# A ring of their own for the late experts' outputs, in a two-layer metaformer kernel on one core

## The chip, the core and the metric

The kernel runs on one core of a Trainium2 chip. A core has five engines with queues of their own: the tensor engine (PE; its weight loads are shown apart as PEld), the vector engine (DVE), the scalar engine (ACT), GpSimd (POOL) and the sync engine (SP), which here only issues transfers. Sixteen DMA engines move data between the chip's memory and the core's working memory. Each engine works through its instructions in the order in which the program gives them, and waits on semaphores for the others.

The metric is the time of one execution in device microseconds, as the median of the runs shown. A profiled execution gives the trace.

## The reference

The input is 32 images of 56 x 56 tokens with 128 channels. Two layers follow each other, each with a mixing step and a step of experts, and each adds its result to the tokens:

```
# layer 0
x = x + conv3x3(sign(batchnorm(ln(x))), sign(W) * scale)          # 128 -> 128 channels
t = t + sum over the 2 best of 8 experts of gate * (ln(t) @ expert_w[e] + expert_b[e])
# layer 1
a = sigmoid((y @ Wa1 + ba1) * (y @ Wa2 + ba2));  b likewise         # y = ln(x), 16 channels
z[i, j, c] = sum over k of a[i, k, c] * b[k, j, c]                  # per image and channel
x = x + sigmoid(y @ Wg + bg) * (ln(z) @ Wz + bz)
# experts that choose tokens: 64 experts, each takes the 8 best tokens of each image
logits = ln(t) @ gate_w.T + gate_b;  probs = softmax over the tokens of an image
top 8 tokens per image and expert, weights topv
pooled = sum over the 8 of topv * token
o = gelu([pooled, 1] @ weight1[e]) ; o = [o, 1] @ weight2[e]
t[chosen token] += topv * o
```

The last step is the one that matters here. An expert makes one output row of 128 numbers per image, and this row, times eight weights, is added to eight tokens of that image. Two experts may choose the same token, so additions to one image's tokens must follow each other.

## The kernel before, in words

**Tiles and stages.** A unit is 896 tokens, held as 128 partitions x 7 x 128 numbers (448 KB). Two images make a pair of seven units; there are sixteen pairs. A first pass over all units (`fetch1`, `stats1`, `norm1`) gathers the batch statistics and stores the turned, normalised units. Then each pair passes through convolution (`sign`, `conv`, `conv_back`), the eight gated experts (`moe_turn`, `moe_route`, `moe_gates`, `moe_experts`, `moe_add`), the product of a and b (`tri_turn`, `tri_b`, `tri_a`, `tri_z`, `tri_out`) and the choice of tokens (`gate_stats`, `gate_turn`, `gate_logits`, `top8`, `pool_rows`). Consecutive pairs overlap.

**The gated experts.** `moe_experts` handles one seventh of a unit. SP loads the eight gates, spread over the partitions, into a tile of 512 KB (L821, tag `gb`, five of them). DVE multiplies the tile by the turned tokens `xT` (L827), and PE multiplies it by the eight experts' weights into one bank (L832). `moe_add` adds the bank to the tokens (L844). A turned unit `xT` is alive from `moe_turn` until its seventh multiply.

**The late experts.** `late_experts` handles four of the 64 experts of the last step at a time, in sixteen groups, and is run twice: with `alone` false for the first thirteen pairs, whose choices are known while the last three pairs are still being worked on, and with `alone` true for the last three pairs, at the end. A group loads its weights (L1412, L1414), multiplies (L1479), turns (L1503), applies gelu (L1519), multiplies again (L1525), adds the bias (L1533) and stores four rows of outputs per image (L1541). For the first thirteen pairs the rows are then loaded again, each repeated eight times, so that one partition holds one chosen token's row (L1551). The images are split into two lots, one of 14 and one of 12 images, so a load covers 112 or 96 partitions. A tile of outputs holds the four experts of a group for one lot. DVE multiplies the whole tile by the weights (L1558), and POOL adds each expert's rows to the output in memory by an indirect transfer that accumulates (L1575). Within a lot each of these 64 transfers waits for the one before; between lots POOL puts a small memset (L1316).

**The rings.** Every tile belongs to a tag, and a tag has a fixed number of buffers in a ring. Tokens `x` have 15, turned units `xT` have 4, `gb` has 5. The outputs of the late experts take `xT` buffers, so do some of the late experts' weights in the last stage; other weights go to `x` and `gb` buffers, and the first fourteen `alone` experts use other memory that has become free by then (`places`).

**The order.** The program doesn't give its instructions in the order in which its stages are written. Every stage puts operations into a list, with an engine, an estimated time, what it reads and writes, and for a transfer how long it takes to land (`land`). The table `TICK` gives each stage of a pair its place within a period of 14. The planner `Order.run` then walks through a modelled time: an engine that is free takes the operation of lowest place whose inputs are there and whose tiles have a buffer. The order that comes out is fixed in the program, queue by queue; on the chip, engines only wait for each other. So a change of `land`, of the rings or of `TICK` can move instructions on all queues and in all pairs.

Of the kernel before, what the change touches and what calls it, by code (L numbers as in the profile page):

```python
# [17 lines left out]
ALU = mybir.AluOpType  # L18
# [9 lines left out]
C = 128  # L28
N7 = 7
UT = N7 * 128  # L30
NU = 7
# [7 lines left out]
    "fetch": (1.58, 3.45, 5.52, -1.97, 9.89, 8.41, 11.94),  # L39
    "sign": (-0.24, 0.69, 0.62, 6.29, 6.36, 10.44, 7.52),  # L40
    "conv": (1.26, 2.47, 6.82, 8.46, 10.49, 11.27, 13.74),
    "conv_back": (3.04, 3.74, 6.89, 9.11, 10.54, 11.48, 14.87),
    "moe_turn": (4.55, 4.08, 9.93, 10.17, 12.05, 12.07, 15.21),
    "moe_gates": (7.93, 6.46, 10.3, 10.32, 15.22, 13.8, 15.72),
    "moe_experts": (10.11, 8.23, 10.44, 10.38, 15.35, 13.82, 17.26),
    "moe_add0": (14.4, 13.58, 10.89, 13, 17.91, 16.49, 17.47),
    "moe_add1": (12.35, 12.05, 11.31, 12.55, 16.09, 14.74, 18.98),
    "tri_turn": (16.03, 16.94, 19.18, 18.34, 19.2, 18.97, 19.62),
    "moe_stats": (4.06, 9.6, 11.95, 15.11),
    "moe_route": (6.11, 10.25, 12.5, 15.67),  # L50
    "tri_stats": (14.43, 14.07, 18.68, 19.34),
    "tri_b": (20.52, 21.37),
    "tri_a": (22.17, 21.41),
    "tri_z": (22.19,),
    "tri_out": (23.45, 23.11, 25.14, 25.06, 25.81, 28.13, 29.03),
    "gate_stats": (23.81, 25.31, 26.89, 30.24),
    "gate_turn": (25.22, 25.8, 26.84, 28.27, 29.66, 32.16, 31.08),
    "gate_logits": (26.8, 27.15, 28.55, 30.19, 30.4, 34.44, 34.71, 34.72),
    "clear": (32.94,),
    "top8": (36.55,),  # L60
    "pool_rows": (39.18,),
    "late_first": (27.19, 27.47, 30.26, 33.5, 37.45, 38.24, 40.16, 41.35, 43.38, 44.86, 45.85,
        48.06, 49.55, 51.3, 58.28, 60.22),
    "late_alone": (47.43, 50.82, 50.84, 53.47, 61.88, 67.39, 57.81, 65.6, 63.21, 71.67, 75.8,
        82.21, 97.17, 84.67, 68.82, 79.34),
    "last_sums": (70.63, 74.49, 77.96),
    "last_load": (68.66, 101.21),
    "last_rows": (91.82, 76.74, 99.71, 103.42, 119.45, 116.33),
# [4 lines left out]
NX, NY = 15, 6  # L73
# [212 lines left out]
def kernel(ctx: ExitStack, tc: tile.TileContext, a: dict, out: bass.AP):  # L286
    nc = tc.nc
# [117 lines left out]
    with ExitStack() as c2:  # L405
# [184 lines left out]
        def fetch(p, u):  # L590
# [3 lines left out]
            @op("SP", 360, w=parts(x_), land=1200)  # L594
            def _():
                nc.sync.dma_start(x_.ap, x_units[g])
# [1557 lines left out]
```

## Time and profile before

| what | value |
|---|---|
| median of 3 runs | 3786.38 us (3786.0 to 3797.89) |
| profiled execution | 3805.24 us |
| its span, first to last instruction | 3803.4 us |
| PE busy | 3427.8 us (90%) |
| DVE busy | 3191.5 us (84%) |
| ACT busy | 2350.5 us (62%) |
| POOL busy | 443.8 us (12%) |
| mean DMA rate | 221 GB/s |

The sum of the prediction is made against the profiled execution, and the difference is carried over to the median. In the profile, a group of instructions is named by its line, engine, operation, and output and input tiles. A wait is given as who waited, for whom, how many microseconds in total, how many times, and the longest. "SPq" and "DVEq" are the queues' own instructions; a DMA named as releaser is a transfer that had to land. A row of the timeline starts with its start and length in microseconds, and ends, in brackets, with the idle time of the engine before it and what ended it. In a matmul row of 32-bit data each matmul is counted twice. The granted clock is that of PE, 1.00 being full speed. The profile marks some idle time "issue", for which it shows no wait.

### The profile page before, as it was taken

To read this page: it belongs to the slowest core of one execution; us is meant where nothing else is said; L and a number is where in the kernel's file an instruction comes from. 1 tells how busy PE (TensorE), PEld (TensorE's weight loads), DVE (VectorE), ACT (ScalarE), POOL (GpSimd) and SP (SyncE) were. 2 spreads that over 40 slices of the span, in tenths; PEclk is the share of its full clock that TensorE was granted. 3 is DMA by queue.
4 is the path that set the end of the run, shared out by engine and by line. 5 is a ranking of instruction groups with operands and counts; after the bars stand their busy time and mean duration, and the time that the engine had idled before them with its cause. 6 is when DMAs were issued, how large, how long until landed. Compare 5 with 4: busy or idle time off the path is not lost.

```text
span 3803.4 us, 79485 instructions
## 1 busy us (share of the span) xinstructions
PE 3427.8 (90%) x28051; PEld 2791.8 (73%) x28051; DVE 3191.5 (84%) x10626; ACT 2350.5 (62%) x5438; POOL 443.8 (12%) x506
## 2 busy tenths in 40 slices
PE   7998999999999999999999999999999997876644
PEld 7886878787877777777777777777777775664422
DVE  7997979898989898989898989898989886765551
ACT  6997357575757666666666666666666664453420
POOL 0000000101010101010101010101010104234454
PEclk9999999999999999999999999999999998898667
DMA  7996747474747474747474747474747477687685
GB/s 292 358 356 226 256 155 268 151 272 148 276 150 268 146 268 153 269 154 269 154 269 156 265 155 268 157 267 158 265 160 262 163 251 210 201 248 227 184 238 163
DMA packets 358127, 842.03 MB, mean 221 GB/s; under 512 B 89169, under 2 KB 133154, under 8 KB 357730
## 3 DMA queue, kind: packets, MB, share of 16 engines
q1 hardware_dynamic: 298658, 719.02, 54.8%
q10 hardware_dynamic: 38080, 99.57, 6.6%
q0 software_dynamic: 20992, 18.37, 2.9%
q8 instruction: 223, 3.65, 0.4%
q14 instruction: 174, 1.43, 0.1%
HBM read 661.53 MB, written 175.23 MB: 220 GB/s over the span
## 4 chain that ended last, share of the span: by engine, by line
PE 44%; DVE 27%; DMA 14%; ACT 8%; issue 3%; SPq 2%; POOL 1%; another core or an unknown queue 0%; ACTq 0%; POOLq 0%; DVEq 0%
PE acc L832 21%; DMA gb<-gate 7%; DVE gb L827 5%; DVE stln L488 5%; PE gram L1799 4%; PE ps_cv L633 4%; PE tr L477 3%; PE ps_g L1067 2%; ACT yt L562 2%; DVE frame L611 2%; DVE x L575 2%; DMA w_True<-in_L_ffn_weight 2%; PE ps_z L976 2%; DVE x L1111 1%; DVE sg L1102 1%
## 5 line engine op out<-in xcount | busy, mean ns | idle before, releaser
L832 PE MATMUL acc<-expert_w,gb 128*128 128x128 f32 x12544 | 1473.6, 278 | 73.0 <-DVE gb L827 49.2
L832 PEld LDWEIGHTS acc<-expert_w,gb 128*128 128x128 f32 x12544 | 1437.7, 193 | 121.7 <-DVE gb L827 51.4
L827 DVE TENSOR_TENSOR gb<-gb,xT 128x1024 f32<-128x1024 f32 x784 | 949.3, 1220 | 95.3 <-DMA gb<-gate 91.3
L488 DVE BATCH_NORM_STATS2 stln<-x 128x6 f32<-128x128 f32 x2352 | 600.1, 287 | 1.9
L562 ACT ACTIVATE yt<-x,rmln 128x128 f32<-128x128 f32 x784 | 327.2, 495 | 203.6 <-DVE rmln L550 190.0
L562 ACT ACTIVATE yl<-x,rmln 128x128 f32<-128x128 f32 x756 | 324.2, 494 | 175.7 <-DVE rmln L547 125.3
L633 PE MATMUL ps_cv<-frame,w_sign 128*128 128x448 bf16 x2016 | 420.0, 357 | 8.3 <-DVE frame L611 8.3
L562 ACT ACTIVATE ym<-x,rmln 128x128 f32<-128x128 f32 x784 | 324.6, 486 | 66.9 <-DVE rmln L550 57.3
L633 PEld LDWEIGHTS <-w_sign 128*128 128x128 bf16 x2016 | 196.5, 98 | 174.4 <-DVE frame L611 8.5
L1222 POOL DMA_INDIRECT rows<-y,near x128 | 133.2, 1041 | 995.5 <-DVE k L738 795.7
L1575 POOL DMA_INDIRECT out<-eo_False,picked x128 | 198.1, 1548 | 317.1 <-DMA out<-eo_False,picked 137.0
L1118 POOL MEMSET a_bd<- 128x2048 f32 x15 | 27.1, 1807 | 1655.4 <-PE ps_zo L1089 1655.4
L562 ACT ACTIVATE y<-x,rm 128x128 f32<-128x128 f32 x448 | 210.5, 716 | 14.5 <-DVE rm L547 14.5
L1067 PE MATMUL ps_g<-wg,yT 128*128 128x128 f32 x1568 | 211.2, 283 | 0.0
L1067 PEld LDWEIGHTS ps_g<-wg,yT 128*128 128x128 f32 x1568 | 192.0, 195 | 20.5 <-issue 12.0
L583 ACT COPY xT<-trm 128x512 f32<-128x512 f32 x224 | 110.1, 529 | 151.6 <-PE trm L477 132.7
L641 ACT ACTIVATE cv<-ps_cv,cv_shift,cv_scale 128x448 f32<-128x448 f32 x224 | 159.2, 726 | 70.7 <-PE ps_cv L633 36.1
L844 DVE TENSOR_TENSOR x<-acc,x 128x512 f32<-128x512 f32 (+1 forms) x224 | 139.7, 623 | 73.7 <-PE acc L832 62.8
L1799 PE MATMUL gram<-y 128*128 128x128 f32 x1568 | 198.4, 279 | 0.0
L1799 PEld LDWEIGHTS gram<-y 128*128 128x128 f32 x1568 | 194.4, 200 | 0.5 <-issue 0.5
L488 DVE BATCH_NORM_STATS2 st<-x 128x6 f32<-128x128 f32 x784 | 179.6, 282 | 4.6 <-DMA x<-in_x 4.6
L583 ACT COPY ylT<-trl 128x512 f32<-128x512 f32 x224 | 113.7, 533 | 111.4 <-PE trl L477 102.0
(263 smaller groups left out, 5439.5 us busy)
## 6 DMA issues: line engine op xcount, KB each, us to landing
gb<-gate SPq DMA_DIRECT2D x784, 512.0 KB
x<-in_x SPq DMA_DIRECT2D x224, 448.0 KB
y<-yT SPq DMA_DIRECT2D x112, 448.0 KB
ys<-y SPq DMA_DIRECT2D x112, 448.0 KB
out<-x ACTq DMA_DIRECT2D x105, 448.0 KB
y<-yl ACTq DMA_DIRECT2D x105, 448.0 KB
w_False<-in_L_ffn_weight SPq DMA_DIRECT2D x128, 256.0 KB
w_True<-in_L_ffn_weight SPq DMA_DIRECT2D x102, 256.0 KB
```

Source lines behind the costliest of these rows:

```text
L488: nc.vector.bn_stats(st.ap[:, c0 + k, :], src.ap[:, k, :])
L562: nc.scalar.activation(dst.ap[:, k, :], src.ap[:, k, :], AF.Identity, bias=m, scale=r)
L583: nc.scalar.copy(t.ap[:, n0 : n0 + k, :].rearrange("c n p -> c (n p)"), ps.ap[:, : k * 128],)
L633: nc.tensor.matmul(acc, lhsT=w_sign[:, tap, :], rhs=frames[f][:, 8 * band + kh : 8 * band + kh + 8, kw : kw + W], start=(tap == 0), stop=( ...
L641: nc.scalar.activation(cv.ap[:, :, 64 * h : 64 * h + 64], ps.ap[:, :448].rearrange("c (q n) -> c n q", n=N7), AF.Identity, bias=cv_shift, ...
L827: nc.vector.tensor_tensor(gb.ap, gb.ap, over(xT.ap[:, n, :], E0), ALU.mult)
L832: nc.tensor.matmul(acc.ap[:, n % 4 * C : (n % 4 + 1) * C], lhsT=gb.ap[:, e, :], rhs=expert_w[:, e * C : (e + 1) * C], start=(e == 0), stop ...
L844: nc.vector.tensor_tensor(dst, acc.ap[:, : k * C], dst, ALU.add)
L1067: nc.tensor.matmul(psg.ap[:, n * C : (n + 1) * C], lhsT=yT[:, n0 + n, 16 * u : 16 * u + 16, :].rearrange("c r v -> c (r v)"), rhs=wg, star ...
L1222: nc.gpsimd.indirect_dma_start(out=rows.ap[:, j, :], out_offset=None, in_=y3_d[p], in_offset=bass.IndirectOffsetOnAxis(ap=near.ap[:, k + j ...
L1575: ins = nc.gpsimd.indirect_dma_start(out=tokens_out, out_offset=bass.IndirectOffsetOnAxis(ap=picked[lot][:rows, e : e + 1], axis=0), in_=e ...
L1799: nc.tensor.matmul(gram.ap[:, :C], lhsT=y.ap[:, n, :], rhs=y.ap[:, n, :], start=(g % G16 == 0 and n == 0), stop=(g % G16 == G16 - 1 and n ...
```

## The change

Four things are changed together.

- The outputs of each late expert get a tile of their own, [128, 2, 128] numbers, 1 KB per partition, with both lots in it, under a new tag `eo` with eight buffers. So a group has four tiles with two loads each, in place of two tiles with four loads each. DVE multiplies each expert and lot by itself, with one weight per partition, so there are 128 multiplies of 128 elements in place of 32 of 512. The 128 accumulating transfers stay.
- Token tiles `x` go from 15 buffers to 14, turned units `xT` from 4 to 3.
- Many estimates of `land` are changed.
- `TICK` has new values in every row, and the order of all queues is drawn up anew from it.

The instructions of PE stay the same in kind and number. The core of the diff:

```diff
 TICK = {
-    "fetch": (1.58, 3.45, 5.52, -1.97, 9.89, 8.41, 11.94),
-    "sign": (-0.24, 0.69, 0.62, 6.29, 6.36, 10.44, 7.52),
-    "conv": (1.26, 2.47, 6.82, 8.46, 10.49, 11.27, 13.74),
+    "fetch": (-0.52, 2.15, 5.26, -2.24, 9.7, 8.97, 10.97),
+    "sign": (-0.11, 0.84, 1.3, 6.88, 7.6, 9.29, 7.72),
+    "conv": (1.51, 1.9, 7.02, 8.48, 10.38, 10.64, 13.69),
...
-NX, NY = 15, 6
+NX, NY, NEO = 14, 6, 8
...
-            "x": NX, "u": NY, "ps": 8, "gb": 5, "xT": 4, "yl": 3,
+            "x": NX, "u": NY, "ps": 8, "gb": 5, "xT": 3, "yl": 3, "eo": NEO,
...
-            @op("SP", 360, w=parts(x_), land=1200)
+            @op("SP", 360, w=parts(x_), land=1262)
...
-            @op("SP", 360, r=[("gd", p, u)], w=[gb], land=1300)
+            @op("SP", 360, r=[("gd", p, u)], w=[gb], land=1392)
...
-            @op("SP", 360, r=[pt], w=[("pooled", p)], land=1500)
+            @op("SP", 360, r=[pt], w=[("pooled", p)], land=5600)
...
-                @op("SP", 360, r=[] if alone else [("ph", name)], w=[second_w[j][1]], land=700)
+                @op("SP", 360, r=[] if alone else [("ph", name)], w=[second_w[j][1]], land=868)
...
-            for lot in () if alone else (0, 1):
-                i0, i1 = LOTS[lot]
-                rows = (i1 - i0) * K1
-                eo = new("xT", [128, N7, C], f"eo_{name}_{lot}")
-
-                @op("SP", 720, r=[("o_d", g)], w=[eo], land=300)
-                def _(eo=eo, i0=i0, i1=i1, rows=rows):
-                    for j in range(NE):
+            for j in () if alone else range(NE):
+                eo = new("eo", [128, 2, C], f"eo_{name}_{j}")
+
+                @op("SP", 720, r=[("o_d", g)], w=[eo], land=800)
+                def _(j=j, eo=eo):
+                    for lot in range(2):
+                        i0, i1 = LOTS[lot]
                         nc.sync.dma_start(
-                            eo.ap[:rows, j, :],
+                            eo.ap[: (i1 - i0) * K1, lot, :],
                             o_d[g][j, i0:i1, :].unsqueeze(1).to_broadcast([i1 - i0, K1, C]),
                         )
-                @op("DVE", 600, r=[("picked", p) for p in range(i0 // 2, i1 // 2)], w=[eo])
-                def _(eo=eo, lot=lot, rows=rows):
-                    nc.vector.tensor_tensor(
-                        eo.ap[:rows, :NE, :], eo.ap[:rows, :NE, :],
-                        along(gains[lot][:rows, es], C), ALU.mult,
-                    )
-
-                for j in range(NE):
+                for lot in range(2):
+                    i0, i1 = LOTS[lot]
+                    rows = (i1 - i0) * K1
+                    e = g * NE + j
+
+                    @op("DVE", 200, r=[eo] + [("picked", p) for p in range(i0 // 2, i1 // 2)],
+                        w=[(eo, lot)])
+                    def _(eo=eo, lot=lot, rows=rows, e=e):
+                        nc.vector.tensor_scalar(
+                            eo.ap[:rows, lot, :], eo.ap[:rows, lot, :],
+                            gains[lot][:rows, e : e + 1], None, ALU.mult,
+                        )
                     @op(
-                        "POOL", 2000, land=4000,
+                        "POOL", 2000, land=4200,
...
-                            in_=eo.ap[:rows, j, :], in_offset=None, compute_op=ALU.add,
+                            in_=eo.ap[:rows, lot, :], in_offset=None, compute_op=ALU.add,
```

The other changes of `land`: transfers of a whole unit 1200 to 1262; the store of z 300 to 1150 and its loads back 300 to 800; the late experts' weights 700 to 868 (two at a time 1400 to 1736), their pooled tokens 300 to 450, their bias 100 to 450, the store of their outputs 200 to 450.

## The prediction

> **What bounds the kernel now.** I read the windows first, then the waits of the tensor engine in two stretches, then the waits of the queue and of the vector engine in the late one, then the timeline of one event there.
>
> The windows answer, for the late stretch up to the last pair's token choice, for the rest, and for twelve pairs in the middle (columns: stretch and its length; busy us and instructions of PE, PEld, DVE, ACT, POOL; granted clock; DMA share; GB/s):
>
> ```profile
> 3100.00:3652.00 552.00, 393.98 (x3110) 297.80 (x3106) 333.84 (x1038) 273.00 (x548) 209.81 (x235) 0.82 0.75 221
> 3652.00:3804.00 152.00, 73.12 (x753) 40.20 (x752) 50.38 (x154) 20.68 (x34) 73.83 (x110) 0.72 0.64 179
> 700.00:3000.00 2300.00, 2207.16 (x18188) 1810.91 (x18187) 2101.43 (x6599) 1507.32 (x3375) 146.41 (x126) 1.00 0.60 211
> ```
>
> In the middle PE is the bound: 2207 of 2300 us, clock 1.00. One pair takes 191.8 us (from the first z product of one pair, at 2052.25, to that of the next, at 2244.05), so it loses 92.8 / 12 = 7.7 us. DVE at 2101 is close behind. From 3100 on no engine is full: PE idles 158 us before 3652 and 79 us after it.
>
> PE's waits in the middle (700 to 3000 us; total us, times, longest):
>
> ```profile
> PE acc L832 <- DVE gb L827: 18.6, 28, 1.3
> PE trg L797 <- DVE k L779: 14.4, 11, 1.4
> PE acc L832 <- DVE q_ln L517: 13.3, 12, 1.1
> PE tr_b L477 <- ACT lines L903: 12.6, 12, 1.1
> PE tr_a L477 <- ACT lines L903: 10.2, 24, 0.7
> PE ps_z L976 <- issue: 7.9, 12, 0.7
> PE trg L797 <- DVE gg L783: 7.1, 14, 0.8
> ```
>
> Nearly all of a pair's loss is PE waiting for DVE's gated copies (2.7 us), for the gates (1.8 us), and around the turned a/b lines (2.6 us). These places repeat in every pair, so a new order moves them thirteen times.
>
> The late stretch, first SP's waits, then DVE's (from 3050 us), then one event:
>
> ```profile
> SPq L1551 <- DMA out<-eo_False,picked: 51.3, 7, 9.7
> ```
> ```profile
> DVE eo_False L1558 <- DMA eo_False<-o: 51.6, 17, 13.1
> DVE gb L827 <- DMA gb<-gate: 31.7, 25, 3.4
> ```
> ```profile
> 3150.91 1.61 POOL L1575 DMA_INDIRECT out<-eo_False,picked  x1 [4.07 <-DMA out<-eo_False,picked]
> ...
> 3154.71 3.18 SPq L1551 DMA_DIRECT2D eo_False<-o  x4
> ...
> 3159.75 0.69 DVE L1558 TENSOR_TENSOR eo_False<-eo_False,gains 96x512 f32<-96x512 f32 x1 [7.49 <-DMA eo_False<-o]
> ...
> 3163.49 2.93 PE L832 MATMUL acc<-expert_w,gb 128*128 128x128 f32 x12 [8.97 <-DVE gb L827]
> ```
>
> A scatter keeps its turned tile; the next load of expert outputs waits for it in SP's queue; DVE, which works in its written order, waits 7.5 us for that load; PE then waits 9.0 us for the gated copy that stood behind it on DVE.
>
> **The change, part by part.** PE gets the same instructions, so only waits move.
>
> *The ring of eight.* In the changed order each group's eight output loads stand together on SP, and a tile is reused two groups later. Groups stand about 32 us apart (ph_False runs from 3105.2 to 3582.8, 16 groups). Scatters that alternate between the lots start every 2.3 us (seven from 3219 to 3233 in the timeline) to 4 us (five from 3178 to 3194), so a group's eight take 18 to 32 us, and the slot wait of 51.3 us on SP mostly goes. I add PE's waits between 3100 and 3652 that stand behind a DVE wait for outputs or a late load: 8.97, 4.23, 1.87, 3.04, 6.68, 5.24, 3.10, 2.86 for DVE or the gates, 3.72 and 2.77 for late-expert weights: 42.5 us. Not all returns. SP still issues 128 output loads at 0.78 us median, but now eight in a row (6.2 us; with the five weight loads put behind them in places, 8.4). Five gated tiles cover 5 x 1.8 us of products less about 3.3 us for a load to land, 5.7 us; so about 2.7 us is uncovered at each of some six groups that stand among gate loads: +16. PE also waits for other things at the same places. I take -19; ends -42 and 0.
>
> *The gains.* 32 multiplies of 512 elements (690 ns) become 128 of 128. The nearest row is L1240, a one-operand scalar multiply of 128 elements: 286 to 351 ns. 128 x 0.29 to 0.35 = 37 to 45 us against 22, +15 to +23 us of DVE over 560 us in which it idles about 40%: +2, ends 0 and +8. [...]
>
> [...] The row: scatters of 1404 to 2972 ns, median 1463. [...]
>
> *14 token tiles, 3 turned tiles.* Twelve pairs already spend 344 us of SP in L596 waiting for a token tile; gate loads stand behind. With 14, that grows. Cover: PE runs on with loaded tiles while SP waits, and DVE's waits for gate loads total 49.5 us in the middle, of which PE felt at most the 18.6 above. Between 0 and +4 us a pair; I count it with the order. In the last stage, weight homes fall from 15 + 4 + 2 x 5 = 29 to 27. In SP's order 96 loads of the last stage stand behind the near-row store, 93 before. Three of 256 KB at 235 GB/s (3600 to 3700) are +3 us; ends 0 and +8. Two more activation-table loads and 15 more of POOL's small memsets are within +2; I take +1.
>
> *The order of a pair.* I count the work queued on each engine between two hand-overs, with trace durations.
>
> (a) In the changed order the gated experts of units 2 and 3 run among the gate products of the previous pair. From the return of unit 5's first conv half to the multiply of the fourth tile of unit 3, DVE holds 6 gated multiplies (1.14 us back to back), 21 statistics (0.20), 8 gate multiplies (2.4 in all), 2 token sums (1.0), 2 returns (1.1), a sign (1.2) and about 21 small steps (0.08): 19.4 us. PE holds there 5 products (1.8), 21 gate matmuls (0.25), 14 of zo (0.095) and 3 transposes (0.11): 15.9. With 0.4 us of hand-over PE waits 3.9. Now the like place costs 1.1 + 1.3 = 2.4 (waits at 2105.26 and 2136.06).
>
> (b) From the return of the next pair's unit 0 to unit 5's first tile: DVE 11 statistics, four returns and a multiply, 5.9 us with hand-over; PE 3.1: 2.8. The same count on the order before gives 2.9 where the trace has 0.77 + 0.57; between the ends 1.3 and 2.8 I take 2.2.
>
> (c) Gates: from the router's transposes of units 0 and 1 to their gate transposes PE has 6.3 us (was about 15), DVE's queued route 7.3: 1.4 with hand-over. The others fall to about 0.2. 1.6 against 1.8.
>
> (d) Lines: seven tiles' products (12.6 us) now stand between the a transposes and z, so of 2.6 us only the b turn's 1.2 stays. z's own chain shrinks with PE's cover (DVE puts two multiplies into it, not six): 0.
>
> Sum per pair 3.9 + 2.2 + 1.6 + 1.2 + 0.3 for small ones = 9.2. The measured kinds were 86.6 / 12 = 7.2. So +2.0 a pair, thirteen pairs: +26; ends -1 and +5 a pair, -13 to +65.
>
> *Sum.* +26 - 19 + 2 + 1 + 3 = +13 us. The profiled execution took 3805.24 us (span 3803.4, 1.8 around it): 3818 there. The median of the runs is 3786.38, 18.9 lower; I carry the difference over: **3799 us**.
>
> **Rivals.** *The late stretch decides (faster).* The freed SP and DVE queues give back all 42 us between 3100 and 3652, and PE's waits per pair grow only by 0.8, because counts like (b) came out too high on the order before. 3786 - 42 + 10 + 5 = 3759. It decides as soon as the pair costs less than 1.5 us more. For it: the 9.0 us event. Against it: (a), where 3.5 us of DVE work has no cover.
> *The ring fills too (same).* Scatters stay behind, outputs wait for tiles of their own ring near the end, where the order splits a group's loads into twos; half of the late gain goes, and the pair is level: near 3786. For it: POOL's 137 us of waits for scatters.
> *Fourteen token tiles hold SP (much slower).* SP stands in L596 ahead of gate loads, and a pair costs +4: 52 - 19 + 6 = +39, 3825. Against it: five tiles ahead cover 5.7 us.
>
> **How the numbers follow.** A run of this kernel is told from no change at about 0.3%, 11 us. The forecast case (3790 to 3810) gets 0.38, of which 0.08 lies within 0.3%; the late stretch 0.36; same 0.10; held SP 0.16. So faster 0.36, same 0.18, slower 0.46. The range takes in all cases with a tenth off each end: 3748 to 3828.
>
> **What would show it.** The pair's period 193 to 195 us instead of 191.8, with PE's waits for gated copies near 6 us a pair in place of 2.7, the largest just after the first gate products; SP's wait for scatters under 15 us, DVE's for outputs under 20; PE idle before the last pair's choice about 20 us less than 158; the end after it some 3 us longer. A period of 191 or less makes the forecast wrong, and the time then falls to the first rival; DVE waits for outputs still near 50 us would make the late gain wrong.

## The result, and the profile after

The changed kernel takes 3849.32 us (median of 4 runs, 3845.69 to 3855.6), the kernel before 3792.14 us beside it (3786.0 to 3800.17): a ratio of 1.0139, 95% interval 1.0109 to 1.017. It is 57 us slower. The forecast was 3799 us, with a range of 3748 to 3828: slower was named as the likeliest sign, but the size was missed and the time lies outside the range.

The profiled execution after has a span of 3844.6 us, against 3803.4 before: 41.2 us. I cut both spans at the first z product of each pair, as the prediction did for one pair:

| stretch of the span (us) | before | after | difference |
|---|---|---|---|
| start to the first pair's z product | 524.1 | 539.7 | +15.6 |
| the thirteen pairs that follow | 2484.3 | 2560.4 | +76.1 |
| from pair 13's z product to the end | 795.0 | 744.5 | -50.5 |

The cut is not quite like for like. Ahead of a z product the new order has done seven gated products more and two halves of a convolution less than the old one (in the first pair six and two; PE has 77 matmul records more before the first z product and 92 fewer behind the last cut). At 1.8 us for a product and 1.9 for a half this is some 7 us of PE's work that has moved into the first row and some 9 us out of the last. So about half of the +15.6 is this shift, and the late part is shorter by some 41 us rather than 50. The middle row, from z to z, holds the same work but for one product.

The period is 197.0 us on average (194.5 to 198.6) where it was 191.1 (189.6 to 193.2). The windows of these thirteen pairs, first before and then after (length; busy us and instructions of PE, PEld, DVE, ACT, POOL; granted clock; DMA share; GB/s):

```profile
524.07:3008.39 2484.32, 2385.56 (x19639) 1958.27 (x19639) 2265.99 (x7128) 1623.99 (x3635) 152.73 (x130) 1.00 0.60 211
```
```profile
539.67:3100.08 2560.41, 2408.85 (x19657) 1998.52 (x19656) 2274.35 (x7137) 1642.63 (x3638) 152.68 (x130) 0.98 0.59 205
```

PE has the same work. Its idle time grew from 98.8 to 151.6 us, 4.1 us a pair, and its busy time by 23.3 us, 1.8 a pair, because the granted clock fell from 1.00 to 0.98: the trace has 78.5 us at half clock in these pairs, against 6.8 before. These two make the 5.9 us of a pair. The window that answers to the prediction's middle one:

```profile
700.00:3000.00 2300.00, 2166.19 (x17679) 1793.89 (x17676) 2044.88 (x6459) 1469.57 (x3247) 140.93 (x120) 0.98 0.58 203
```

The prediction's two late windows would hold other work than before, since everything stands about 90 us later there. PE's waits of the changed kernel from 700 to 3000 us (total, times, longest), 11.7 pairs:

```profile
PE acc L832 <- DVE gb L827: 45.2, 39, 2.4
PE trt L477 <- ACT d L774: 20.7, 9, 2.3
PE trt L477 <- ACT yt L562: 16.5, 14, 2.3
PE trm L477 <- ACT ym L562: 11.6, 11, 1.1
PE ps_l L1162 <- ACT ylT L583: 10.8, 11, 1.0
PE ps_zo L1089 <- ACT a_bd L1055: 7.9, 12, 0.7
PE trc L477 <- ACT cv L641: 7.2, 12, 0.6
PE tr_a L477 <- ACT lines L903: 4.4, 7, 0.8
PE acc L832 <- DVE mk L734: 3.0, 8, 0.4
```

The waits for the gates (`trg`) and for the b lines (`tr_b`), 34 us before, are gone. The waits of the gated products for DVE (`acc`) went from 2.7 to 4.1 us a pair. New are six rows that wait for ACT: the normalised tiles `yt` and `ym`, the sigmoids `d`, `ylT`, `a_bd` and the conv copies `cv`. They sum to 74.7 us, 6.4 a pair; before, the only one of them in the list was `cv` with 0.3 us. A row names the engine that came last: how much of these 6.4 us is ACT's own time is not shown, since ACT waits too.

Where one of the largest starts, in the timeline of one pair after:

```profile
2465.83 3.48 DVE L1193 FIND_INDEX8 i<-m,lgT 128x8 uint32<-128x3136 f32 x1
...
2469.93 2.90 ACT L1206 ACTIVATE lgT<-lgT,sq 128x3136 f32<-128x3136 f32 x1
...
2476.47 0.88 ACT L562 ACTIVATE yt<-x,rmln 128x128 f32<-128x128 f32 x2 [1.72 <-DVE rmln L550]
...
2477.98 1.28 ACT L773 ACT_TABLE_LOAD   x1
...
2479.50 2.02 ACT L562 ACTIVATE yt<-x,rmln 128x128 f32<-128x128 f32 x5
...
2480.03 0.86 PE L477 MATMUL trt<-ident,yt 128*128 128x128 f32 x2 [2.30 <-ACT d L774]
```

DVE searches the chosen tokens' indices (3.48 us) ahead of unit 6's statistics, so ACT waits 1.72 us for DVE and the normalised tiles start late; ACT makes two of seven, then loads a table and runs the two sigmoids of the next pair's route, and only then the other five. PE waits 1.06 us and 2.30 us around it.

What such a wait did to the clock here depended on where it fell. PE waits for the fourth gated tile of unit 3 in every pair, 2.44 us each time. Two pairs, the wait and the group behind it:

```profile
2158.95 5.47 PE L832 MATMUL acc<-expert_w,gb 128*128 128x128 f32 x32 [2.44 <-DVE gb L827]
1963.05 3.84 PE L832 MATMUL acc<-expert_w,gb 128*128 128x128 f32 x32 [2.44 <-DVE gb L827]
```

All half-clock stretches of these pairs, 22 of them, start on one grid of 3.41 us and last one step of it (one lasts two). Along this grid, two other pairs with the same wait, which ends at 2357.43 in the first block and at 983.08 in the second:

```profile
2353.80:2357.22 3.42, 1.19 (x11) 0.99 (x9) 3.42 (x14) 2.42 (x7) 0.00 (x0) 1.00 0.91 323
2357.22:2360.63 3.41, 3.20 (x15) 3.20 (x16) 2.45 (x10) 1.90 (x5) 0.00 (x0) 0.50 0.89 354
```
```profile
978.22:981.64 3.42, 2.43 (x22) 2.23 (x21) 3.42 (x20) 1.18 (x4) 0.00 (x0) 1.00 0.57 219
981.64:985.05 3.41, 1.97 (x17) 1.97 (x18) 3.27 (x10) 2.48 (x7) 0.00 (x0) 1.00 1.02 416
985.05:988.46 3.41, 3.41 (x39) 3.17 (x39) 3.34 (x7) 2.80 (x7) 0.00 (x0) 1.00 0.95 352
```

Where most of the wait falls into one step, PE is busy for 1.19 of 3.42 us (35%), and the next step runs at half clock; where it is divided between two steps (71% and 58% busy), none does. All 22 full-clock steps with PE busy for 47% or less are followed by half clock, and none of the 704 with 48% or more. The wait at unit 3 has a half-clock step behind it in nine of thirteen pairs, where the group takes 5.35 to 5.47 us (7.25 for a longer group in the first pair), and none in four, where it takes 3.84. The two waits around 2480 have one in all thirteen. The nine pairs with both take 197.6 us on average, the four with one 195.5: a half-clock step at unit 3 costs about 2 us. DVE is full, or nearly so, until the wait ends (3.42 of 3.42 us in the first block; 3.42 of 3.42 and 3.27 of 3.41 in the second). The kernel before has two such steps in all thirteen pairs.

Late, SP's wait for scatters was 51.3 us. The like row now, and DVE's and POOL's waits, from 3050 us on:

```profile
SPq L1550 <- DMA out<-eo_False,picked: 1.1, 3, 0.5
POOL out L1578 <- DMA out<-eo_False,picked: 73.4, 31, 6.2
DVE eo_False L1565 <- DMA eo_False<-o: 41.3, 33, 7.7
DVE gb L827 <- DMA gb<-gate: 26.3, 21, 5.1
```

### The profile page after: what moved, and what is told of

It is laid out like the page before. It is cut to its first block, busy times and chain, and to the rows that moved or that the text cites. A ratio compares the mean times of both kernels' runs of the same rounds, so it can differ in the third digit from the quotient of the medians.

```text
span 3844.6 us, 79480 instructions
## 1 busy us (share of the span) xinstructions
PE 3434.8 (89%) x28051; PEld 2818.9 (73%) x28051; DVE 3209.4 (83%) x10722; ACT 2372.0 (62%) x5440; POOL 443.7 (12%) x521
## 3 DMA queue, kind: packets, MB, share of 16 engines
q14 instruction: 175, 1.43, 0.1%
## 4 chain that ended last, share of the span: by engine, by line
PE 43%; DVE 28%; DMA 10%; ACT 9%; issue 4%; POOL 1%; SPq 1%; another core or an unknown queue 0%; ACTq 0%; POOLq 0%; DVEq 0%
PE acc L832 22%; DMA gb<-gate 6%; DVE gb L827 6%; DVE stln L488 5%; PE gram L1802 3%; PE ps_cv L633 3%; DVE sg L1102 3%; PE tr L477 2%; DVE frame L611 2%; DVE x L1111 2%; ACT ym L562 1%; ACT cv L641 1%; PE ps_z L976 1%; DVE i L1193 1%; PE ps_l L1162 1%
## 5 line engine op out<-in xcount | busy, mean ns | idle before, releaser
L832 PE MATMUL acc<-expert_w,gb 128*128 128x128 f32 x12544 | 1503.9, 280 | 99.0 <-DVE gb L827 78.8
L832 PEld LDWEIGHTS acc<-expert_w,gb 128*128 128x128 f32 x12544 | 1457.1, 195 | 162.7 <-DVE gb L827 87.8
L488 DVE BATCH_NORM_STATS2 stln<-x 128x6 f32<-128x128 f32 x2352 | 550.6, 283 | 2.5
L1067 PE MATMUL ps_g<-wg,yT 128*128 128x128 f32 x1568 | 203.4, 280 | 0.0
L1077 ACT ACTIVATE sg<-ps_g 128x512 f32<-128x512 f32 x224 | 118.3, 536 | 122.8 <-PE ps_g L1067 116.5
```

The costliest lines, as they stand in the source:

```text
L488: nc.vector.bn_stats(st.ap[:, c0 + k, :], src.ap[:, k, :])
L832: nc.tensor.matmul(acc.ap[:, n % 4 * C : (n % 4 + 1) * C], lhsT=gb.ap[:, e, :], rhs=expert_w[:, e * C : (e + 1) * C], start=(e == 0), stop ...
L1067: nc.tensor.matmul(psg.ap[:, n * C : (n + 1) * C], lhsT=yT[:, n0 + n, 16 * u : 16 * u + 16, :].rearrange("c r v -> c (r v)"), rhs=wg, star ...
L1077: nc.scalar.activation(sg.ap[:, n0 : n0 + k, :].rearrange("p n c -> p (n c)"), psg.ap[:, : k * C], AF.Sigmoid,)
```

## The experiments

Theories to begin with: A, the order costs the pairs and the ring pays late; B, the scarcer token and turned tiles cost the pairs. All ratios below are to the kernel before on the same chip. The stretches (us) are those of the table above, each from one profiled execution. late_sigmoid, sign_later and filled, which start from the changed order, have its shift of 7 to 9 us in their first and last figures; the held runs have before's amount of work on both sides, rings_only behind the last cut. The late figures are good to some 10 us: late_sigmoid and sign_later take 754 where the changed kernel, with nearly the same late order, takes 744.5.

| run | ratio, 95% interval | start to first z | 13 pairs | from pair 13's z on |
|---|---|---|---|---|
| rings_only | 1.0207 (1.0188 to 1.0225) | 537.1 | 2566.1 | 750.0 |
| order_only | 1.0406 (1.0388 to 1.0424) | 533.1 | 2608.6 | 785.2 |
| mix13 | 1.0396 (1.0373 to 1.0419) | 537.4 | 2666.1 | 727.9 |
| both_moves | 1.0685 (1.0659 to 1.0711) | 540.7 | 2770.9 | 731.8 |
| held_14_3_8 | 0.9998 (0.9985 to 1.0012) | 539.3 | 2480.6 | 776.2 |
| held_15_3_5 | 0.9978 (0.9963 to 0.9992) | 536.5 | 2481.4 | 774.5 |
| late_sigmoid | 1.0138 (1.0119 to 1.0157) | 542.1 | 2562.0 | 753.7 |
| sign_later | 1.0117 (1.0095 to 1.0139) | 540.3 | 2550.5 | 754.5 |
| filled | 1.0097 (1.0069 to 1.0126) | 548.3 | 2546.4 | 738.2 |
| splice_after_13 | 0.9929 (0.9905 to 0.9952) | 539.0 | 2497.8 | 723.0 |
| splice_mix_13 | 0.9938 (0.9913 to 0.9964) | 534.9 | 2495.5 | 730.2 |
| splice_after_14_4_5 | 1.0071 (1.0047 to 1.0095) | 521.2 | 2498.9 | 812.4 |

### The table and the rings apart

**rings_only**: the changed kernel with the ticks and landing times of before.

```diff
 TICK = {
-    "fetch": (-0.52, 2.15, 5.26, -2.24, 9.7, 8.97, 10.97),
+    "fetch": (1.58, 3.45, 5.52, -1.97, 9.89, 8.41, 11.94),
...
-            @op("SP", 360, w=parts(x_), land=1262)
+            @op("SP", 360, w=parts(x_), land=1200)
...
```

> The rings of the change (14 token tiles, 3 turned tiles, 8 tiles of outputs, with the split loads and multiplies) under the ticks and landing times of before. Theory A, the order table costs the pairs and the ring of eight pays late: the pair's period stays near 191 to 193 us instead of 197, and the part after the thirteenth pair's z product is 20 to 50 us shorter than before's 795 us; time near 3740 to 3790. Theory B, the scarcer token and turned tiles cost the pairs (SP and PE wait for tiles): period 195 to 198 and a time of 3830 to 3860, as in the changed kernel.

Neither theory fits as it stands: 3854.69 us. The planner, given other rings, drew another order. The first nine pairs take 196 to 207 us and the last four 190.4 to 191.5. These are the windows of the last three pairs and of two slow ones:

```profile
2530.68:3103.12 572.44, 548.98 (x4536) 452.08 (x4537) 525.05 (x1647) 375.06 (x841) 35.13 (x30) 1.00 0.60 212
1340.49:1746.95 406.46, 379.83 (x3003) 306.30 (x3002) 349.95 (x1111) 252.10 (x561) 23.11 (x20) 0.97 0.56 195
```

PE idles 7.8 us a pair in the former, as before the change, with the clock at 1.00, and 13.3 us in the latter, with 0.97. So 14 token tiles and 3 turned ones allow 191 us, and what differs between these pairs is the order. The late part is 45 us shorter than before's, with before's ticks and before's amount of work in it: it is as good as the changed kernel's.

**order_only**: the kernel before with the ticks and landing times of the change. The edit is shown against the changed kernel.

```diff
-NX, NY, NEO = 14, 6, 8
+NX, NY = 15, 6
...
-            "x": NX, "u": NY, "ps": 8, "gb": 5, "xT": 3, "yl": 3, "eo": NEO,
+            "x": NX, "u": NY, "ps": 8, "gb": 5, "xT": 4, "yl": 3,
...
```

> The ticks and landing times of the change on the rings of before (15, 4, outputs in turned tiles). Theory A: the period is near 197 us as in the changed kernel, +76 us over thirteen pairs, and most of the late gain is missing because a scatter still holds its turned tile; 3850 to 3900. Theory B: the period falls back to 191 to 193 and the time lies near 3790 or lower.

A's numbers, and more: pairs of 201 us on average (185.5 to 206.7) and a late part only 10 us shorter than before's. It is no clean test of a fixed order either, since the planner drew it anew for these rings.

**mix13**: the changed kernel, with two tables.

```diff
         def put(p, name, i, stage, *args, add=0.0):
-            plan.append((at(p, TICK[name][i] + add), len(plan), stage, args))
+            table = TICK_NEW if p >= 13 or name.startswith(("late", "last")) else TICK
+            plan.append((at(p, table[name][i] + add), len(plan), stage, args))
```

> The changed kernel with the ticks of before for pairs 0 to 12 and its own for pairs 13 to 15 and for all late and last rows. Theory A: head and middle as before (period 191 to 193, +0 to +25 us), the end keeps its gain of about 50 us; 3735 to 3770, faster than both kernels. Theory B: period 195 to 198 here too, 3820 to 3850. If the late gain belongs to the ticks of the middle (work of pairs 11 and 12 done earlier), the end falls back to about 795 us and the time to about 3790.

A miss of both: the pairs lie between 195 and 219 us. Only the end, 727.9 us, is short. Ticks and rings can't be judged apart as long as the planner stands between them. This order loses behind DVE's gates, as before's did, and behind ACT's normalised tiles, as the changed one does (mix13, PE's waits from 745 to 3000 us):

```profile
PE trg L830 <- DVE gg L816: 43.3, 20, 5.4
PE trt L510 <- ACT yt L595: 23.6, 13, 7.2
```

### The order held still

For the next two the order of before is not drawn but written out as a list of the operations, and the rings and the outputs' code of the change are put under it.

```diff
     def run(self):
+        ops = self.ops
+        steps = struct.unpack(f"<{len(ops)}h", zlib.decompress(base64.b64decode(GIVEN)))
+        out = list(itertools.accumulate(steps))
...
```

> All of the change but its order: 14 token tiles, 3 turned tiles, eight tiles of outputs with their loads and multiplies, in the order of before, which is written out as a list; PE's list differs from before's in 36 of 8511 rows. An operation whose tile is not free yet moves back until it is; the eight loads of a group stand together. Theory C, the order alone costs the pairs: the period is 191 us in all thirteen pairs, and the part after the thirteenth pair's z product is about 45 us shorter than before's 795, as in the run with rings alone (750); time near 3740, faster than both kernels. Rival, 14 token tiles or 3 turned tiles cost by themselves: the period is 193 us or more, or the head grows by over 5 us.

> The same with 15 token tiles, 3 turned tiles and five tiles of outputs, which fit in the same memory. Theory C: period 191 us. If the count of token tiles matters in the pairs, this run is shorter in the middle than the one with 14 by its cost; if eight tiles of outputs matter against five, its late part is longer, by up to 20 us. If neither, both lie near 3740.

```profile
539.27:3019.82 2480.55, 2385.80 (x19638) 1958.34 (x19639) 2266.04 (x7127) 1621.58 (x3635) 153.26 (x130) 1.00 0.61 211
```
```profile
536.47:3017.91 2481.44, 2385.88 (x19639) 1958.59 (x19639) 2266.14 (x7128) 1622.79 (x3635) 152.62 (x130) 1.00 0.61 211
```

The first row is the thirteen pairs with 14 token tiles, the second with 15. They agree within 1 us and lie 3 to 4 us below before's 2484.3: under this order the rings cost the pairs nothing. Theory B falls, and the 76 us belong to the order. Theory C's late number fell too: not 45 us but 19 to 20 (776.2 and 774.5 against 795.0). DVE's wait for outputs in the run with eight tiles, against 51.6 before:

```profile
DVE eo_False L1627 <- DMA eo_False<-o: 32.0, 17, 10.7
```

With five tiles (and 15 token tiles) it is 43.4 us, and the late part is as long; since both counts differ, opposite effects could cancel here. And both runs spend 12 to 15 us more before the first z product, which eats what the late part gives.

### Moves within the changed order

These take the changed kernel's finished order and move a few operations in every pair. The helper puts the chosen operations, and what depends on them, behind an anchor:

```diff
+    def later(self, out, chosen, anchor):
+        held, head, end = set(), [], out.index(anchor)
+        for k in out[: end + 1]:
+            if chosen(k) or not held.isdisjoint(self.ops[k][4]):
+                held.add(k)
+            else:
+                head.append(k)
+        return head + [k for k in out[: end + 1] if k in held] + out[end + 1 :]
```

**both_moves**:

```diff
+        for p in range(2, 14):
+            index = self.of("DVE", "top8", p - 1)[1]
+            norms = self.of("ACT", "tri_turn", p, 6)[:7]
+            out = self.later(out, lambda k: k == index, max(norms, key=out.index))
+        for p in range(1, 14):
+            gated = self.of("DVE", "moe_experts", p, 2, 2)[0]
...
+            out = self.later(out, lambda k: k in back, gated)
```

> The changed kernel with two moves in its finished order, in every pair: the index search of the token choice (3.5 us of DVE, with the exponential behind it) goes behind the last normalised tile of unit 6, and two gated multiplies of units 3 and 2 go ahead of the gate statistics that stand before them. If the 2.3 us waits for the normalised tiles and for the gated copy, each with one stretch at half clock behind it, are what a pair lost (2.4 + 1.06 + 2.3 of wait and about 1.7 for each half-clock stretch), the period falls from 197 to 190 to 193 us, the granted clock in the middle goes from 0.98 to 1.00, and the time falls by 50 to 90 us to 3760 to 3800. If the delayed search only carries the wait to the next consumer of DVE and ACT, the period stays within 1.5 us of 197 and the waits appear under other names.

The clearest miss: the period is 213 us on average, 215 in most pairs. PE's waits from 700 to 3000 us:

```profile
PE tr_a L520 <- ACT lines L946: 95.9, 10, 10.1
PE ps_b L933 <- ACT yT L897: 50.9, 10, 5.1
PE acc L875 <- ACT yl L605: 44.7, 11, 4.6
```

and the cause of the first two, from the timeline:

```profile
2412.48 3.42 DVE L1236 FIND_INDEX8 i<-m,lgT 128x8 uint32<-128x3136 f32 x1
...
2416.19 2.89 ACT L1249 ACTIVATE lgT<-lgT,sq 128x3136 f32<-128x3136 f32 x1
...
2419.08 0.56 ACT L897 COPY yT<-trt 128x512 f32<-128x512 f32 x1
...
2419.70 4.15 PE L933 MATMUL ps_b<-yT,wb 128*32 128x448 f32 x20 [5.09 <-ACT yT L897]
```

The exponential, moved with the search, now stands ahead of the copies that the b lines need, and the gathers that wait for the indices hold DVE's weighted sums and with them the a lines (10.1 us). The statistics put behind the gated multiplies come out as a wait of 4.6 us two tiles later (the row names ACT; DVE's gated multiply ended just before PE went on). The waits were carried on, and dearer.

**late_sigmoid** and **sign_later** move far less:

```diff
+        for p in range(2, 14):
+            sigmoids = self.of("ACT", "moe_route", p, 0)[1]
+            out = self.later(out, lambda k: k == sigmoids, self.of("PE", "tri_b", p - 1, 0)[1])
```
```diff
+        for p in range(1, 14):
+            sign = self.of("DVE", "sign", p + 1, 0)[0]
+            out = self.later(out, lambda k: k == sign, self.of("DVE", "moe_experts", p, 2, 2)[0])
```

> The changed kernel with one move in every pair: the two sigmoids of the route of units 0 and 1, with the table load before them and the gates that follow from them, go behind the copies of unit 6's turned tiles. Theory D, PE's wait for the normalised tiles behind that table load, and the half-clock stretch after it, are part of what the pair lost: the 2.3 us wait of the turned tiles on the sigmoids goes, the period falls by 2 to 4 us to 193 to 195, time 3800 to 3825. Rival, ACT and DVE are only late at this place and what is moved is waited for next (gates, turned lines): the period stays within 1 us of 197 or grows, and the wait stands under the gates or the gated copies.

> The changed kernel with one operation moved in every pair: the sign of the next pair's unit 0 (1.23 us of DVE) goes behind the gated multiply of the third tile of unit 2. The 2.44 us wait for the fourth tile of unit 3 falls to about 1.2; if the half-clock stretch after it goes too, the period falls by 2.5 to 3 us (to 194, time near 3812), if it stays, by 1.2 (195.7, time near 3834). If DVE is short of time over the whole stretch of gate products and not at this tile, the 1.2 us come back at the next gated copies and the period stays at 197.

With the sigmoids moved the wait behind them goes and comes back at the gates, and the period is 197.1 as before the move: the rival's case. So taking ACT's load and sigmoids out of this place gained nothing. One pair of it:

```profile
2484.39 0.71 PE L512 MATMUL trt<-ident,yt 128*128 128x128 f32 x2 [1.10 <-ACT yt L597]
...
2491.55 0.38 PE L832 MATMUL trg<-ident,gg 128*56 128x128 f32 x2 [1.94 <-DVE gg L818]
```

With the sign moved, one pair:

```profile
2353.13 3.84 PE L867 MATMUL acc<-expert_w,gb 128*128 128x128 f32 x32 [1.43 <-DVE gb L862]
...
2358.66 5.60 PE L867 MATMUL acc<-expert_w,gb 128*128 128x128 f32 x48 [1.04 <-ACT yl L597]
```

1.43 + 1.04 us in place of 2.44: the 1.2 us moved away are waited for two tiles later, so DVE is short of time over the stretch and not at one tile (the second row names ACT, but a gated multiply of DVE, begun at 2357.30, ended just ahead of it). Yet the period fell to 196.2, and PE's first group took 3.84 us where it took 5.35: the clock stays at 1.00 here, in all thirteen pairs, with two short gaps for one long. Over the thirteen pairs:

```profile
540.31:3090.76 2550.45, 2398.98 (x19657) 1984.05 (x19655) 2273.78 (x7137) 1642.02 (x3638) 152.83 (x130) 0.99 0.60 206
```

PE idles 151.5 us, as in the changed kernel (151.6), and is busy 9.9 us less with the same instructions: the whole gain, 0.8 us a pair, is the clock's, with 51.2 us at half clock in place of 78.5. It is read from one trace of each kernel: the intervals of their total times overlap.

### The clock by itself

**filled** adds work to PE only.

```diff
+                        again = 7 if n0 + n == 1 and name.startswith("trt_") and name.endswith("_6") else 1
+                        for _ in range(again):
...
+                for _ in range(16 if (u, n) == (3, 3) else 0):
+                    nc.tensor.matmul(
+                        acc.ap[:, n % 4 * C : (n % 4 + 1) * C], lhsT=ident,
+                        rhs=expert_w[:, :C], start=True, stop=True,
+                    )
```

> The changed kernel in its own order, with work added for PE alone at the two places of a pair where it waits and the clock then halves: six more transposes of a tile that is there already while it waits for unit 6's normalised tiles, and sixteen products that are overwritten at once while it waits for the fourth gated tile of unit 3. No other engine gets anything. Theory E, the granted clock is a loss of its own, set off by PE standing idle: both stretches of half clock go, the clock of the middle returns from 0.98 to 1.00, and the period falls by 2 to 3 us to 194 to 195 although PE has 3.4 us more work in each pair; time 3810 to 3825. Rival, the clock in the records only follows PE's idle share and costs nothing by itself: the period stays within 0.5 us of 197 or grows.

PE has over 30 us more busy time in the thirteen pairs (2441.9 against 2408.9 us) and they take 14 us less (195.9 us each); the ratio of the total times is lower too, though its interval just overlaps that of the changed kernel. The place of unit 3's fourth tile in one pair:

```profile
2355.92 1.73 PE L1074 MATMUL ps_g<-wg,yT 128*128 128x128 f32 x14
2357.48 3.74 PE L834 MATMUL acc<-expert_w,ident 128*128 128x128 f32 x32
2361.05 3.74 PE L839 MATMUL acc<-expert_w,gb 128*128 128x128 f32 x32
```

The useless products take 3.74 us, more than the wait of 2.44 us that they fill. Still the stretch from the gate product's start to the end of the gated group is shorter, 8.9 us against 9.5, because the gated group behind runs 3.74 us at full clock and not 5.35. At unit 3 no half-clock step is left in any of the thirteen pairs. At the other place the six transposes were too short: 0.66 us for a gap of 2.3, and 1.64 us of it remain. In ten of the thirteen pairs a half-clock step still follows, 37.5 us in all, where the changed kernel had 47.8 us at this place. In one pair it lasts two steps.

So 1.1 us a pair came of the 2 to 3 forecast. The direction is theory E's: the clock was a cost of its own here, set off by PE standing idle, for more work on PE, and nothing else, made the pairs shorter. Its whole share of the 5.9 us is not measured; the growth of PE's busy time puts it at 1.8.

### The best of both

**splice_after_13** and **splice_mix_13**: the list of the held order as far as pair 13's z product, then what is left in the changed order, or in that of mix13.

> The order of before (held, with the rings of the change) up to the z product of pair 13, and from there what is left in the order of the changed kernel. Theory C: head and thirteen pairs as in the held run (3020 us to the z product of pair 13), the rest as in the changed kernel (745 us, against 776 with the order of before there): 3760 to 3775, faster than both kernels by 0.7 to 1.2%. If the late gain is owed to what the changed order has done by pair 13 already, the rest takes 760 to 780 us and the time stays near 3795.

> The same, with the end of the order that was drawn up from the ticks of before to pair 12 and those of the change from pair 13 on; that order's own run was slow in the pairs, but its part after the thirteenth pair's z product was the shortest of all, 728 us. Theory C: 3020 + 728 + 2, 3745 to 3765. If its end was short only because its pairs were slow and loads had landed early, the rest takes 745 us or more and the time is 3765 or above.

3761.25 and 3762.26 us: 0.7% and 0.6% faster than before and over 2% faster than the changed kernel. At the seam 47 operations that the changed order has done by then are still to do, and the pair that crosses it takes 207 us; behind it the end takes 723 us. Counted from pair 12's z product, ahead of the seam, the remaining time is 986.5 us before, 967.4 in the held order with the ring, 943.1 in the changed kernel, 930.3 in this one. So the ring alone gives 19 us, and a late order drawn for the ring 37 more in the splice, where the cut is like for like (24 in the changed kernel, where it is not). The shorter end of mix13 (727.9) didn't carry over as an advantage.

**splice_after_14_4_5**: the same with other rings.

```diff
-NX, NY, NEO = 14, 6, 8
+NX, NY, NEO = 14, 6, 5
...
-            "x": NX, "u": NY, "ps": 8, "gb": 5, "xT": 3, "yl": 3, "eo": NEO,
+            "x": NX, "u": NY, "ps": 8, "gb": 5, "xT": 4, "yl": 3, "eo": NEO,
```

> The spliced order (before's up to the z product of pair 13, the changed one's from there) with 14 token tiles, four turned tiles and five tiles of outputs, which take the same memory; what finds no tile of outputs free moves back (66 operations, late). Theory F, the 10 to 15 us that every run with three turned tiles spent more before the first z product (534 to 540 us against 524) come from the first pair, where before keeps a fourth turned tile and the route has to wait without it: the head returns to about 524 us and the time falls by 10 to 15 us to 3745 to 3755 if five tiles of outputs do no harm late, to 3760 or more if they do. Rival, the head differs between executions and not by the tiles: it stays at 534 us or more.

The start comes back: 521.2 us. The windows of 400 to 450 us, before, with three turned tiles (held_15_3_5) and with four in this run:

```profile
400.00:450.00 50.00, 48.04 (x408) 43.96 (x407) 45.73 (x132) 12.56 (x33) 0.00 (x0) 1.00 0.72 249
```
```profile
400.00:450.00 50.00, 43.01 (x356) 40.41 (x353) 41.52 (x105) 8.67 (x22) 0.00 (x0) 0.97 0.59 205
```
```profile
400.00:450.00 50.00, 48.45 (x412) 44.38 (x411) 46.53 (x138) 13.17 (x34) 0.00 (x0) 1.00 0.72 245
```

With three, PE gets 43 us of work done in these 50, not 48. In the pairs of before's written order a fourth turned tile is live in the first one and then not again until the last stage; without it the first pair's routes had to move back. The time is 3830.48 us all the same, since the order was drawn for eight tiles of outputs, and five hold it up late, 812 us in place of 723:

```profile
DVE eo_False L1631 <- DMA eo_False<-o: 129.5, 47, 11.5
```

Its DVE waits for outputs are 129.5 us, against 36.2 in splice_after_13. How many tiles of outputs are needed depends on the order above them: in before's, five were enough. A version that keeps four turned tiles in the first pair and eight tiles of outputs late wasn't tried.

## Why the prediction was wrong

**The sum.** It put the profiled execution at 3818 us; it took 3846.46, 28 more. By the terms: the pairs were +76, not +26 (50 more); the late part was -50 where the ring, the gains, the tables and the last stage made -13 (38 less); the start, which had no term, +16 (with the shift of 7 to 9 us at the cuts: late about -41, start about +8). Then 18.9 us were taken off because the profile of before lay that far above its median; after, the profile lies 2.9 us below its median, so this step added 22 us to the miss. Runs of the kernel before on other chips had medians of 3778.8 to 3802.9 us: the offset belonged to the run, and shouldn't have been carried over.

**The order of a pair (+2.0 us a pair; measured +5.9).** This is the step that failed. The sum put PE's waits at +2.0 us and the clock at nothing; measured are +4.1 us of idle time and +1.8 us of slower work. In the terms of the sum: *(a)* and *(b)*, 6.1 us of waits for gated copies, came to 4.1. *(c)* and *(d)*, 2.8 us together, were to stay, and only 0.4 is left of them: the new order does remove what it was counted to reduce. Waits behind ACT, which the sum did not have, came to 6.4. It counted the work queued on DVE and PE between two hand-overs, and on ACT nothing, though ACT has a table load of 1.28 us between two normalised tiles. The waits of the profile before showed only DVE in this role, apart from the lines, and I took the list of engines from the old order into the new one. That the pair is limited by ACT itself does not follow: ACT also passes on DVE's lateness, and with its load and sigmoids moved away the period stayed at 197.1.

*(a)* was right in place, the largest wait just behind the first gate product, and moving the sign shows DVE short of time there. (Its items give 19.4 us with 1.0 us for each of the two token sums.) The wait is 2.44 us where 3.9 was said. With 1.6 us of half clock in nine of thirteen pairs the place costs 3.6 us; that this is near 3.9 is luck, since the sum had no clock in it.

**The clock.** The prediction read 1.00 in the middle and let it stand, and gave a forecast wait of 3.9 us no second price. Its own windows have a lower clock where PE idles more: 1.00 with PE busy for 96% of the middle, 0.82 with 71% and 0.72 with 48% late. That single gaps within a pair can do this, before's middle hardly showed: two half-clock steps in thirteen pairs. In the changed kernel the waits at the two places of a pair, 2.44 and 2.3 us long, were followed by half clock in 22 of 26 cases, for 3.41 us or more each, and all 22 stretches start on one grid of that step.

**The ring (-19; measured -19 to -20 with the order held, about -41 as changed).** Taken alone the term was right to within 2 us, which is in part luck: -19 was chosen between -42 and 0, the late figures are no better than 10 us, and the waits behind it did not go as said. SP's wait for scatters fell to 1.1 us, but DVE's wait for outputs stayed at 41.3 us (32.0 and 43.4 with the order held) and not under 20. And an order drawn for the ring gives 20 us or more on top, which I had no term for. That this is owed to the new ticks is not shown: rings_only, with before's ticks, has the same gain.

**14 token tiles and 3 turned tiles (+3 in the last stage).** The token tiles cost nothing in the pairs: 2480.6 us with 14 and 2481.4 with 15. The rival in which they hold SP falls, although the changed kernel does wait longer for token tiles. The turned tiles cost 11 to 15 us in the held and spliced runs, whose work before the first z product is that of before; but in the first pair, where I hadn't looked: I read twelve middle pairs and the late stretch, and the resource that was cut was used in full only outside them. In the changed kernel's 15.6 us some 7 us are work done earlier; order_only, with four turned tiles and the same shift, spent 9 us more there. The +3 of the last stage could not be told apart.

**The gains (+2).** The held order with 14 token tiles runs all 128 small multiplies, and its late part gained 18.8 us where the ring's term alone was 19; so the dearer multiplies cost little there. In the trace after they take 280 ns in the median, 36 us in all: just under what the row of before gave (37 to 45). The scatters take 1457 ns in the median (at most 2445) beside them, against 1463 (at most 2972) before: POOL shows no loss. No run measured the multiplies apart.

**The rivals.** That the late stretch decides was right about the late stretch (it gave about the 42 us that this rival hoped for) and wrong about the pairs. The splices show what it would have been worth: with pairs at 191 us, 3761.

## What to carry to other kernels

When an order is drawn anew, count the hand-overs of every engine at the places where the cover goes, ACT's table loads (1.28 us each here) among them, and not only those of the engine that the old profile names; then price each remaining gap twice, once as the wait and once for the clock behind it. In the changed kernel's thirteen pairs the gap's length alone did not tell that (2.44 us, with half clock behind it in nine pairs and not in four); the busy share of the 3.41 us step that it fell into did (47% or less: 22 of 22; 48% or more: none of 704). A resource that is cut is looked up where it is used in full, which may be the first pair and not the middle. To judge a ring apart from a planner's order, write the old order out and hold it: three runs in which the planner redrew it told little, and the first one that held it told nearly all.

## What the runs showed of the hardware

In the thirteen pairs of the changed kernel the granted clock changed only on a grid of 3.41 us. A step at full clock in which PE was busy for 47% or less was followed by one at half clock (22 of 22), a step with 48% or more was not (704 of 704). In the kernel before the two sides lie at 47% (two steps) and 54%, in sign_later at 40% and 55%. The same wait of 2.44 us was therefore followed by half clock in nine pairs and not in four, by where it lay on the grid. This border is not all there is to it: in filled it lies at 50 to 53%, and in late_sigmoid some steps with more (up to about 70%) were followed by half clock, and a few with 43 to 46% were not; why is open.

A gap of 1.4 and one of 1.0 us with 4.5 us of work between them, in place of the 2.44 us, were followed by half clock in none of thirteen pairs. Products that nobody reads, 3.74 us of them put into the gap of 2.44 us, took the half-clock steps at this place away in all thirteen pairs and made the pairs shorter.
